# A residual layer with split float32 products: quarters in longer runs over two queues, the bias put into the bank ahead of the products, tiles 2 to 7 turned by VectorE

## The chip, the core and the metric

The kernel runs on one core of a Trainium2 chip. A core has TensorE (the matmul array, which writes into the eight banks of PSUM), VectorE, ScalarE and GpSimd for elementwise work, SyncE, which issues transfers, and 16 DMA engines that all transfers share. Each engine works through its own instructions in order; semaphores hold an instruction until what it needs is done. The metric is the device time of one execution in microseconds (us); of a version, the median of its runs.

## The reference: what is computed

x has shape (4, 1024, 512), the condition (4, 256), W (1536, 512), b (512). Cut to what matters:

```python
hidden = concatenate([cond, cond], -1)                       # (4, 512)
x_mean = mean(x, axis=1, keepdims=True)                      # (4, 1, 512)
fused  = concatenate([x, x_mean * ones, hidden * ones], -1)  # (4, 1024, 1536)
y      = x + relu(einsum('bld,do->blo', fused, W) + b)
```

The einsum falls into three: x times the first 512 rows of W (the large product), the mean of x over the 1024 positions times the next 512 rows, and the condition times the last 512, whose two halves can be added first. The second and third parts and b are the same for all 1024 positions of a row of the batch: they are called the row's bias here. The output is x + relu(product + bias).

## The kernel before

The 4 x 1024 positions are 32 tiles of 128 positions, eight per row. For the product TensorE needs x turned, with the features along the partitions. Tiles are grouped into ten units: tiles 0 and 1 alone, tiles 2 and 3, tiles 4 to 7, and then units of four tiles, two per row. A unit's features come in four pieces of 128 (j = 0 to 3).

*Turning.* Units 0 to 3 (tiles 0 to 7, `BY_PE`) are turned by TensorE: x is loaded with positions along the partitions, and `nc.tensor.transpose` (L261) writes 128x128 blocks into PSUM. The other six units are loaded a second time as "z", in an arrangement (`zv`, L119) that puts each quarter of the features on 32 partitions, so that VectorE's transpose of 32x32 blocks (L267) finishes the turn. A z unit is eight transfers of 128 KB (half h, quarter i, L161), and each of its runs in memory is 64 floats, 256 bytes.

*Splitting.* The product is kept at float32 accuracy by splitting each operand into a float32r part and the rest: `hi` is ScalarE's copy (L278, which also sums over positions for the mean), `lo` is VectorE's or GpSimd's subtraction (L294). W's first part is split in the same way (L237 to L245). For each tile and piece, TensorE then does three matmuls, w_hi x hi, w_hi x lo, w_lo x hi (L439), so 12 per tile, into one of five banks (`O_BANKS`).

*The bias.* ScalarE scales the condition's W rows (L356), GpSimd adds them (L361), ScalarE copies the sum into a bank (L365), VectorE adds four mean terms to it (L368) once the row's sums are there, the result is split (L374, L378), TensorE multiplies it with a matrix of 1/1024 so as to sum over the partitions (L385), and ScalarE copies the row's bias out (L389).

*Finishing.* The first five tiles (`KEEP = 5`) are copied out of their bank by ScalarE before the bias exists (L451), and GpSimd adds the bias later (L457). For the others VectorE adds the bias while it reads the bank (L457), ScalarE applies relu (L460), GpSimd adds x (L463). The last four tiles are done by VectorE alone: bias into the bank (L473), then relu and x in one operation (L468). The last tile is done in two halves of 256 columns. Each tile is stored by L478.

*What sets the order.* The class `Plan` (L18) is a list scheduler that runs while the program is built: every operation has an engine with a cost, the operations it depends on, and a due time; the plan takes the operation that could start first, by due time within a small window, and emits it. So each engine's order, SyncE's order of loads and stores too, comes out of these costs. The due times follow `at(t)`, the time planned for tile t. On the chip each engine keeps that order and waits where data are late. All loads of x, z and W and all stores are issued by SyncE on one queue. Eight semaphores serve the transfers in turn, so a transfer is issued only when the eighth before it has landed.

*The start.* Five matmuls on zeros (L225) run first. Tile 0's x, the first half of W, tile 1's x, the second half of W, the rest of unit x0 and x1, w_mean and w_cond are issued in this order, then the z units.

Of the kernel before, what the change touches and what calls it, by code (L numbers as in the profile page):

```python
# [8 lines left out]
F32 = mybir.dt.float32  # L9
# [8 lines left out]
class Plan:  # L18
# [3 lines left out]
    HANDOVER = 0.2  # L22
    PATIENCE = 0.12

    def __init__(self, engines):
        self.free = dict.fromkeys(engines, 0.0)
        self.todo, self.done, self.log = {}, {}, []

    def add(self, key, costs, deps, due, emit, later=0.0):
        assert key not in self.todo, key  # L30
        self.todo[key] = (costs, list(deps), due, emit, later)

    def run(self):
        while self.todo:
            could = []
            for key, (costs, deps, due, _, _) in self.todo.items():
                if not all(d in self.done for d in deps):
                    continue
                options = []
                for engine, cost in costs.items():  # L40
                    start = self.free[engine]
                    for d in deps:
                        end, later, by = self.done[d]
                        if by != engine:
                            end += later + self.HANDOVER
                        start = max(start, end)
                    options.append((start + cost, start, engine, cost))
                _, start, engine, cost = min(options)
                could.append((start, due, key, engine, cost))
            assert could, list(self.todo.items())[:8]  # L50
            first = min(could, key=lambda t: t[:2])
            start, _, key, engine, cost = min(
                (t for t in could if t[3] == first[3] and t[0] <= first[0] + self.PATIENCE),
                key=lambda t: (t[1], t[0]),
            )
            _, _, _, emit, later = self.todo.pop(key)
            self.log.append((start, engine, key, start - self.free[engine]))
            self.free[engine] = start + cost
            self.done[key] = (start + cost, later, engine)
            emit(engine)  # L60
# [3 lines left out]
def kernel(  # L64
# [8 lines left out]
    nc = tc.nc  # L73
# [11 lines left out]
    S_BUFS = 13  # L85
    T_BUFS = 3
# [3 lines left out]
    O_BUFS = 14  # L90
    KEEP = 5
    BY_DVE = 3
# [3 lines left out]
    STEP, START = 2.82, 6.0  # L96
# [17 lines left out]
    plan = Plan(["pe", "dve", "act", "pool", "sp"])  # L114
    nc_of = {"pe": nc.tensor, "dve": nc.vector, "act": nc.scalar, "pool": nc.gpsimd}
# [3 lines left out]
    zv = x.rearrange("r (n t) (h i c) -> r h i t n c", t=Q, i=NQ, h=2)  # L119
    Wv = W.rearrange("(s h p e) o -> s h p e o", p=P, e=2, h=2)  # L120
# [4 lines left out]
    BY_PE = (0, 1, 2, 3)  # L125
# [8 lines left out]
    in_sbuf = {c for c, (u, js) in enumerate(pieces) if u not in BY_PE and js[0] == 3}  # L134


    xs, zs = {}, {}
# [15 lines left out]
    def x_here(t):  # L153
        return ("x", t // G, t % G) if t < 2 else ("x", 0, 2) if t < G else ("x", t // G)

    def load_z(u, h, i):
        r, k0, n = units[u]
        if not h and not i:
            zs[u] = zpool.tile([P, 2, G * NQ, P // 2], F32, tag="z", name=f"z{u}")
        i = (0, 2, 1, 3)[i]  # L160
        nc.sync.dma_start(  # L161
            out=zs[u][i * Q : (i + 1) * Q, h, : n * NQ],
            in_=zv[r, h, i, :, k0 * NQ : (k0 + n) * NQ],
        )

    def load_w(h):
        nc.sync.dma_start(out=w_x[:, 2 * h : 2 * h + 2], in_=Wv[0, h])

    SP, SPZ = 0.7, 1.3
    clock = 1.9  # L170
    for key in (("x", 0, 0), ("w", 0), ("x", 0, 1), ("w", 1), ("x", 0, 2), ("x", 1)):
        if key[0] == "w":
            load_w(key[1])
            clock += 2 * SP
        else:
            n = 1 if key in (("x", 0, 0), ("x", 0, 1)) else 2 if len(key) == 3 else G
            load_x(key[1], key[2] if len(key) == 3 else 0, n)
            clock += n * SP
        plan.done[key] = (clock, 0.3, "sp")
    plan.free["sp"] = clock  # L180
# [7 lines left out]
    wcs = {}  # L188
    plan.add(("w_mean",), {"sp": 4 * SP}, [("x", 1)], -50, lambda e: nc.sync.dma_start(out=w_mean.rearrange("p (h e) o -> p h e o", h=2), in_=Wv[1].rearrange("h p e o -> p h e o")), later=1.0)
    for n, u in enumerate(by_z):  # L190
        for h in range(2):
            for i in range(NQ):
                deps = [("turn", c) for c in range(len(pieces)) if n >= Z_BUFS and pieces[c][0] == by_z[n - Z_BUFS]]
                due = at(first_tile[u]) - 30 + i + 4 * h if u != 3 else -60
                plan.add(("z", u, h, i), {"sp": SPZ / 2}, deps, due, lambda e, u=u, h=h, i=i: load_z(u, h, i), later=1.0)
    x_order = ["w_x", 0, 1, "cond"] + list(range(2, B * NK // G))
    for n, g in list(enumerate(x_order))[3:]:
# [29 lines left out]
    for _ in range(N_WARM):  # L227
        warm_up()
# [340 lines left out]
```

## Time and profile before

| what | us |
|---|---|
| median of 3 runs (115.6 to 117.58) | 115.7 |
| the profiled execution | 114.52 |
| its span in the profile | 112.7 |
| TensorE busy, matmuls (443) | 102.3 |
| VectorE busy (131 operations) | 73.0 |
| GpSimd busy (62) | 68.6 |
| ScalarE busy (123) | 54.0 |
| transfers, share of the 16 DMA engines' time over the span | 84.6% |
| bytes read and written | 17.83 MB and 8.39 MB |

Busy time of matmuls counts overlapping instructions, each from its start to its modelled end. Successive starts tell the pace better. An idle stretch of an engine is put down to what ended it. Stretches of time are read in slices of the span; a share of an engine or of the transfers there says what that stage was short of. By line, the matmuls of the product are 150 us of such overlapping spans, the transposes by TensorE 6.4, the matmuls of the mean 3.4.

### The profile page before, as it was taken

What the parts mean: (1) busy time and instruction counts of PE and PEld (TensorE: products, weight loads), DVE (VectorE), ACT (ScalarE), POOL (GpSimd) and SP (SyncE); (2) the same over time, 40 slices, a digit from 0 to 9 for tenths busy, and PEclk for the clock granted to TensorE, in tenths of its full rate; (3) what the DMA queues carried; (4) which work ended last, traced back from release to release, by engine and by line L of the source; (5) the groups of instructions that cost most, each with busy time, mean ns of one, the idle gap of its engine ahead of it and who ended that gap; (6) DMA issues with size and microseconds to landing.
All of it is one profiled execution on the core that took longest, in us unless ns stands there. A gap on an engine that the chain in (4) does not pass through costs nothing.

```text
span 112.7 us, 1479 instructions
## 1 busy us (share of the span) xinstructions
PE 102.3 (91%) x443; PEld 80.7 (72%) x443; DVE 73.0 (65%) x131; ACT 54.0 (48%) x123; POOL 68.6 (61%) x62
## 2 busy tenths in 40 slices
PE   5879999999999999989999899999993499999970
PEld 2447888888887888858888588888881488888860
DVE  1299245568969999898975993699049442224470
ACT  5260357799849850999542473662216522220000
POOL 6159007299979999799999948575506744440000
PEclk9999999999999999999999999999999999999997
DMA  3999999999999989999999999999893222224231
GB/s 104 338 351 400 405 331 181 187 133 192 221 317 174 197 229 329 345 215 341 377 257 209 282 386 307 307 310 333 202 333 111 93 93 93 93 93 186 93 128 59
DMA packets 35487, 26.31 MB, mean 233 GB/s; under 512 B 26132, under 2 KB 26392, under 8 KB 35480
## 3 DMA queue, kind: packets, MB, share of 16 engines
q1 hardware_dynamic: 35440, 26.22, 84.6%
q8 instruction: 3, 0.05, 0.2%
q14 instruction: 4, 0.03, 0.1%
q0 software_dynamic: 32, 0.00, 0.0%
q10 hardware_dynamic: 8, 0.00, 0.0%
HBM read 17.83 MB, written 8.39 MB: 233 GB/s over the span
## 4 chain that ended last, share of the span: by engine, by line
PE 35%; POOL 21%; DMA 20%; DVE 9%; issue 5%; ACT 4%; SPq 2%; POOLq 0%
PE po_None L439 26%; DMA out_dram<-o 11%; POOL o L463 10%; DMA z<-in_x_dram 9%; POOL o L457 5%; PE xT L261 4%; POOL cond L361 3%; POOL lo L294 3%; PE po L439 3%; ACT hi L278 2%; PE pw L225 2%; DVE xT L267 2%; SPq L478 2%; DVE w_lo L244 2%; DVE acc L368 1%
## 5 line engine op out<-in xcount | busy, mean ns | idle before, releaser
L439 PE MATMUL po_None<-w_hi,lo 128*128 128x512 f32 x124 | 50.1, 404 | 0.6 <-POOL lo L294 0.6
L439 PE MATMUL po_None<-w_hi,hi 128*128 128x512 f32 x124 | 50.6, 408 | 0.0
L439 PE MATMUL po_None<-w_lo,hi 128*128 128x512 f32 x124 | 49.6, 401 | 0.7 <-DVE w_lo L244 0.7
L463 POOL TENSOR_TENSOR o<-o,x 128x512 f32<-128x512 f32 x28 | 35.8, 1292 | 12.9 <-ACT o L460 8.3
L278 ACT ACTIVATE hi<-xT 128x512 fp32r<-128x512 f32 (+1 forms) x34 | 19.5, 575 | 20.3 <-DVE xT L267 9.7
L439 PEld LDWEIGHTS po_None<-w_lo,hi 128*128 128x128 f32 x124 | 23.7, 191 | 7.1 <-DVE w_lo L244 1.4
L439 PEld LDWEIGHTS po_None<-w_hi,lo 128*128 128x128 f32 x124 | 23.9, 192 | 6.4 <-POOL lo L294 1.0
L439 PEld LDWEIGHTS po_None<-w_hi,hi 128*128 128x128 f32 x124 | 23.9, 193 | 5.3
L294 DVE TENSOR_TENSOR lo<-xT,hi 128x512 fp32r<-128x512 f32 (+1 forms) x28 | 17.9, 643 | 8.3 <-ACT hi L278 8.3
L460 ACT ACTIVATE o<-o 128x512 f32<-128x512 f32 x28 | 16.8, 628 | 11.9 <-DVE o L457 11.9
L267 DVE STREAM_TRANSPOSE xT<-z 128x512 f32<-128x512 f32 x24 | 16.1, 702 | 9.2 <-DMA z<-in_x_dram 7.2
L457 DVE TENSOR_TENSOR o<-po_None,bias 128x512 f32<-128x512 f32 x23 | 15.2, 681 | 9.4 <-POOL o L463 4.2
L368 DVE SCALAR_TENSOR_TENSOR acc<-w_mean,tot,acc 128x512 f32<-128x512 f32 x16 | 12.1, 755 | 0.5
L294 POOL TENSOR_TENSOR lo<-xT,hi 128x512 fp32r<-128x512 f32 x6 | 7.8, 1294 | 4.7 <-ACT hi L278 4.7
L457 POOL TENSOR_TENSOR o<-o,bias 128x512 f32<-128x512 f32 x5 | 6.4, 1310 | 1.0 <-ACT bias L389 1.0
L261 PE MATMUL xT<-ident,x 128*128 128x128 f32 x32 | 6.4, 327 | 0.4 <-DMA x<-in_x_dram 0.4
L261 PEld LDWEIGHTS xT<-ident,x 128*128 128x128 f32 x32 | 5.4, 206 | 1.6 <-DMA x<-in_x_dram 0.8
L347 POOL TENSOR_TENSOR wc<-w_cond 128x512 f32<-128x512 f32 x2 | 2.5, 1287 | 6.6 <-DMA w_cond<-in_L_cond_W_dram 6.6
L361 POOL TENSOR_TENSOR cond<-b_sb,term 128x512 f32<-128x512 f32 x4 | 5.2, 1294 | 2.1 <-ACT term L356 2.1
L278 ACT ACTIVATION_READ_ACCUMULATOR hi<-xT 128x1 f32 x32 | 6.2, 195 | 0.0
L361 POOL TENSOR_TENSOR cond<-cond,term 128x512 f32<-128x512 f32 x4 | 5.2, 1298 | 0.2
L356 ACT ACTIVATE term<-wc,cT 128x512 f32<-128x512 f32 x8 | 5.3, 714 | 0.0
(46 smaller groups left out, 56.2 us busy)
## 6 DMA issues: line engine op xcount, KB each, us to landing
out_dram<-o SPq DMA_DIRECT2D x31, 256.0 KB, 4.4
x<-in_x_dram SPq DMA_DIRECT2D x7, 1024.0 KB, 7.1
z<-in_x_dram SPq DMA_DIRECT2D x48, 128.0 KB, 5.2
w_x<-in_L_cond_W_dram SPq DMA_DIRECT2D x2, 512.0 KB, 4.5
w_mean<-in_L_cond_W_dram SPq DMA_DIRECT2D x1, 1024.0 KB, 10.9
w_cond<-in_L_cond_W_dram SPq DMA_DIRECT2D x1, 1024.0 KB
x<-in_x_dram SPq DMA_DIRECT2D x2, 256.0 KB, 3.2
x<-in_x_dram SPq DMA_DIRECT2D x1, 512.0 KB, 6.3
```

The costliest lines, as they stand in the source:

```text
L261: nc.tensor.transpose(v[:, (m * n + i) * P : (m * n + i + 1) * P], x_t[:, j // 2, j % 2], ident)
L267: nc.vector.transpose(v[:, : n * P].rearrange("p (n t) -> p n t", t=Q), zs[u][:, js[0] // 2, : n * NQ].rearrange("p n (a e) -> p n e a", e ...
L278: nc.scalar.activation(hi[c][:, :m], xT[c][:, :m], AF.Copy, accum_out=sums[:, r, js[0], s : s + 1] if len(js) == 1 else None,)
L294: nc_of[e].tensor_tensor(lo[c][:, :m], xT[c][:, :m], hi[c][:, :m].bitcast(F32), ALU.subtract)
L347: eng.tensor_tensor(wc[:, k], v[:, 0, k], v[:, 1, k], ALU.add)
L356: nc.scalar.activation(terms[r, n], wc[:, n], AF.Copy, scale=cT[:, n, r : r + 1])
L361: nc.gpsimd.tensor_tensor(conds[r], conds[r] if n else bL, terms[r, n], ALU.add)
L368: nc.vector.scalar_tensor_tensor(acc[r], w_mean[:, j, :], totals[r][:, j : j + 1], acc[r], ALU.mult, ALU.add)
L439: nc.tensor.matmul(pos[key][:, :w], lhsT=v[p][:, c], rhs=m[:, j, d], start=(j == 0 and n == 0), stop=(j == J - 1 and n == 2),)
L457: nc_of[e].tensor_tensor(o, o if t < KEEP else pos[t], biases[t // NK], ALU.add)
L460: nc.scalar.activation(outs[t], outs[t], AF.Relu)
L463: nc_of[e].tensor_tensor(outs[t], outs[t], x_tile(t), ALU.add)
```

## The change

The new version keeps the three matmuls per piece and the arithmetic. What differs:

- **z in longer runs.** Features are dealt to pieces in another way: piece j takes features 128 i + 32 j + c, where c counts within 32. A z unit is then four transfers instead of eight, with runs of 128 floats, 512 bytes, and VectorE's transpose reads 32 neighbours per block instead of every second. W's rows are loaded in the same order, as four transfers per part (`load_w`). From unit 4 on, quarters 1 and 3 are issued by ScalarE, on its queue; the others stay with SyncE. The order of all loads is written out (`LOADS`), and each load depends on the load before it on each queue.
- **Tiles 2 to 7 by VectorE.** `BY_PE` holds only tiles 0 and 1. Units 2 and 3 become z units. For tiles 0 and 1 VectorE first copies x into the dealt order (`deal`), in two halves, and TensorE turns the copy.
- **lo.** GpSimd takes the lo of pieces 1 and 3 of every z unit, and all four of unit 2; VectorE takes the rest. w_lo is all VectorE's.
- **The bias ahead of the products.** For tiles 20 to 23 and 26 to 31 (`EARLY`) ScalarE copies the row's bias into the bank first (`preload`), the products add to it without a start flag, and VectorE does relu and x in one operation. Other tiles go as before; `KEEP` is 3 and the parked tiles are finished later.
- **Row 0's bias** begins with the first mean term; the condition's part is added at the end (`acc_end`).
- **Fillers.** Where the plan leaves TensorE idle for over 0.2 us before the condition's transposes, matmuls on zeros of 128 columns are put in: six before tile 0's transposes, eight before the first product, one before tile 2. The condition's transposes move behind tile 2's first piece.
- **The plan** has other costs, models the transfers as one line with bytes, and adds to each due time a shift by kind and a random part from a fixed seed. The buffer counts change.

The diff, cut to its core:

```diff
-    S_BUFS = 13
-    T_BUFS = 3
+    S_BUFS = 14
+    T_BUFS = 4
-    O_BUFS = 14
-    KEEP = 5
-    BY_DVE = 3
+    O_BUFS = 10
+    KEEP, PARKED = 3, 5.0
+    IN_SBUF = {2: (0, 1, 2, 3), 3: (1, 3)}
+    EARLY = (99, 16, 20, 26)
+    TWO, Z_MB = 4, 3.8
+    SEED, SPREAD, SHIFT = 27816, 1.0, {
...
-    zv = x.rearrange("r (n t) (h i c) -> r h i t n c", t=Q, i=NQ, h=2)
-    Wv = W.rearrange("(s h p e) o -> s h p e o", p=P, e=2, h=2)
+    zv = x.rearrange("r (n t) (i f) -> r i t n f", t=Q, i=NQ)
+    Wv = W.rearrange("(s i j c) o -> s j i c o", i=NQ, j=J, c=Q)
-    BY_PE = (0, 1, 2, 3)
+    BY_PE = (0, 1)
-    in_sbuf = {c for c, (u, js) in enumerate(pieces) if u not in BY_PE and js[0] == 3}
+    in_sbuf = {c for c, (u, js) in enumerate(pieces) if u not in BY_PE and js[0] in IN_SBUF.get(u, (1, 3))}
...
-        nc.sync.dma_start(
-            out=zs[u][i * Q : (i + 1) * Q, h, : n * NQ],
-            in_=zv[r, h, i, :, k0 * NQ : (k0 + n) * NQ],
+        nc_of[e].dma_start(
+            out=zs[u][i * Q : (i + 1) * Q, : n * NQ], in_=zv[r, i, :, k0 * NQ : (k0 + n) * NQ]
         )
+    LOADS = [("z", 2), ("z", 3), ("cond",), ("w_mean",), ("z", 4), ("z", 5), ("x", 0), ("x", 1)]
+    for u, g in zip(range(6, len(units)), range(2, B * NK // G)):
+        LOADS += [("z", u), ("x", g)]
+            for i in range(NQ):
+                load(("z", u, i), "act" if i % 2 and u >= TWO else "sp", Z_MB * units[u][2] / 16, frees[v],
+                     at(first_tile[u]) - 22 + i, lambda e, _, u=u, i=i: load_z(e, u, i))
...
+            if not conds_turned and idle > 0.2:
+                for _ in range(int((idle - 0.1) / 0.1)):
+                    warm_up(P)
...
+    def deal(t, h):
+        if not h:
+            dealt[t] = small.tile([P, J, P], F32, tag="term", bufs=TERMS, name=f"dealt{t}")
+        j = slice(h * J // 2, (h + 1) * J // 2)
+        nc.vector.tensor_copy(
+            dealt[t][:, j].rearrange("p j (q c) -> p j q c", q=NQ),
+            x_tile(t).rearrange("p (q j c) -> p j q c", q=NQ, j=J)[:, j],
+        )
...
-            nc.vector.transpose(
-                v[:, : n * P].rearrange("p (n t) -> p n t", t=Q),
-                zs[u][:, js[0] // 2, : n * NQ].rearrange("p n (a e) -> p n e a", e=2)[:, :, js[0] % 2],
+                zs[u][:, : n * NQ, js[0] * Q : (js[0] + 1) * Q],
             )
...
+    def acc_end(r):
+        nc.vector.tensor_tensor(acc[r], acc[r], conds[r], ALU.add)
+    def preloaded(t):
+        return t >= EARLY[t // NK]
+    def preload(t, h):
+        nc.scalar.activation(bank(t, h), biases[t // NK][:, cols(h)], AF.Copy)
...
-                start=(j == 0 and n == 0), stop=(j == J - 1 and n == 2),
+                start=(i == 0 and not preloaded(t)), stop=(i == 3 * J - 1), skip_group_check=preloaded(t),
...
-    def bias_in_bank(t, h=None):
-        nc.vector.tensor_tensor(v, v, biases[t // NK][:, d], ALU.add)
+    def relu_add_x(t, h):
+        d = cols(h)
+        nc.vector.scalar_tensor_tensor(o_tile(t)[:, d], bank(t, h), 0.0, x_tile(t)[:, d], ALU.max, ALU.add)
```

## The prediction, made before the changed kernel was run

> **What bounds the kernel now.** I read the slices first, then TensorE's timeline, then the chain of waits at the one large hole. The slices (40 of 2.82 us):
>
> ```profile
> PE   5879999999999999989999899999993499999970
> PEclk9999999999999999999999999999999999999997
> DMA  3999999999999989999999999999893222224231
> GB/s 104 338 351 400 405 331 181 187 133 192 221 317 174 197 229 329 345 215 341 377 257 209 282 386 307 307 310 333 202 333 111 93 93 93 93 93 186 93 128 59
> ```
>
> TensorE is full but for both ends and one hole near 87 us. The transfers are full too until about 82 us, and at the full share they move 400 GB/s in some slices and 133 to 200 in others: those are the quarters, in runs of 256 bytes. So TensorE sets the end, and where it stops it is for data that came late. Products follow each other at 0.233 us once the array is fast (72 in 16.79 us in the chain that ended last), but not at first:
>
> ```profile
> 8.71 0.63 PE L439 MATMUL po_None<-w_hi,hi 128*128 128x512 f32 x1
> 9.14 0.63 PE L439 MATMUL po_None<-w_hi,lo 128*128 128x512 f32 x1
> 9.57 0.63 PE L439 MATMUL po_None<-w_lo,hi 128*128 128x512 f32 x1
> ...
> 12.59 0.39 PE L439 MATMUL po_None<-w_hi,hi 128*128 128x512 f32 x1
> 12.82 0.39 PE L439 MATMUL po_None<-w_hi,lo 128*128 128x512 f32 x1
> 13.05 0.40 PE L439 MATMUL po_None<-w_lo,hi 128*128 128x512 f32 x1
> ```
>
> Starts lie 0.43 us apart before 12.6 us and 0.23 after, although the column of the granted clock reads 9 throughout. The hole, in time order over all engines:
>
> ```profile
> 76.85 0.42 SPq L161 DMA_DIRECT2D z<-in_x_dram  x1
> 83.41 1.30 DVE L267 STREAM_TRANSPOSE xT<-z 128x512 f32<-128x512 f32 x2 [4.38 <-DMA z<-in_x_dram]
> 85.13 0.40 PE L439 MATMUL po_None<-w_lo,hi 128*128 128x512 f32 x1
> 88.09 0.68 DVE L378 TENSOR_TENSOR acc_lo<-acc,acc_hi 128x512 fp32r<-128x512 f32 x1
> 88.83 0.50 PE L385 MATMUL pb<-acc_hi,mean 128*128 128x512 f32 x1 [3.30 <-DVE acc_lo L378]
> ```
>
> The last quarter of the last unit is issued at 76.85, behind the store of tile 19, which waited for GpSimd; VectorE turns it at 83.41, the last row's mean follows, and TensorE, which takes its work in order, stands before the mean's product (the row reads 3.30; start to start it is 3.70 less one slot, 3.47).
>
> **The sum from the front.** The 25th product (tile 2's first) starts at 16.57 and the last ends at 109.18. From there TensorE has 29 tiles x 12 x 0.2333 = 81.2, the last tile 2.84, twelve transposes at 0.117 = 1.4, four mean products of two slots (1.9), the hole 3.5: 90.8 of 92.6; the other 1.8 are short gaps.
>
> *Start.* Tile 0's x is there by 3.87 (its transposes start). New ahead of them are two half copies on VectorE (a whole 128x512 copy takes 0.43 there, so 0.5 with the gap); then four transposes at the slow 0.27, ScalarE's hi 0.60, and eight filler matmuls of 128 columns (a quarter of 0.43 each, 0.85) that stand in order before the first product: 3.87 + 0.5 + 1.1 + 0.85 = 6.3, against 6.20 now. W in quarters does not bring the first 1.5 MB sooner (ScalarE waited until 7.54 for the last of it, same order of bytes), but w_lo is now all VectorE's: 0.68 each, where one took 1.79 beside GpSimd's. From 6.3 to tile 2 TensorE has 24 products and four transposes. Fast: 24 x 0.2333 + 4 x 0.117 = 6.1, tile 2 at 12.4. Slow until 12.6 as now: 12 products by then, 12 x 0.2333 = 2.8 left, 15.4. The fillers close the gaps that TensorE has now (5.01 to 5.42, 7.40 to 8.12), so I take the middle, 13.9. The rule of the Trainium skill (TensorE: Matmul & The Clock Gate, Part 1) is that about 3.4 us of sustained activity release the clock; the trace is slower than that, being busy from 1.18 with small gaps and slow until 12.6. By the rule tile 2 would start near 12.4.
>
> *Data for tiles 2 to 7.* Now TensorE turns these from x; now 24 transposes fall away, 2.8 us, but their quarters must land early. What does a run of 512 bytes cost? No row shows one. Bounds:
>
> ```profile
> 8.50:14.10 5.60, 5.60 (x21) 4.46 (x21) 3.53 (x6) 1.09 (x4) 2.56 (x2) 1.00 1.03 401
> ...
> 22.50:25.40 2.90, 2.90 (x14) 2.36 (x13) 1.78 (x3) 2.64 (x6) 2.82 (x3) 1.00 0.96 132
> 25.40:28.20 2.80, 2.80 (x13) 2.26 (x13) 2.53 (x4) 2.80 (x9) 2.53 (x3) 1.00 0.91 195
> ```
>
> The last column is GB/s: quarters alone move 132 to 195, say 170; rows of 2 KB and more 345 to 401, say 375. A straight line through time per run (16 engines: 24 ns for 256 bytes, 87 for 2 KB) gives 33 ns for 512, **248 GB/s**; ends 170 and 375. The Trainium skill (DMA: Bandwidth & Descriptors, Specifications) gives 512 B as the least transfer for full rate; by that it is 375 and all below is 2.7 us earlier. Its front page (Trainium Kernel Development and Optimization, Key Constraints) says that a second queue saves issue time alone; no run here shows two.
>
> Unit 3 (tiles 4 to 7): 1.5 MB by 7.5, then units 2 and 3 and the two quarters of unit 4 that ScalarE issues early, 2.0 MB, 8.1 us: 15.6. Its first lo stands on VectorE behind four turns (0.65 each), a sum and totals: 15.6 + 3.4 + 0.7 = 19.7. TensorE reaches tile 4 at 13.9 + 5.6 + 0.3 (condition's transposes, moved here) = 19.8: no wait. Its second lo is GpSimd's, behind the two adds that need w_cond, another 1 MB: 15.6 + 2.8 + two of 1.28 + 1.29 = 22.3; in order TensorE wants it after two slots of three products, 21.2. So **1.3 us of new wait** (handover counted). At 375 none; at 170 the two waits come to 4.7.
>
> *After that.* The transposes (1.4 of them past 16.57), the hole (3.5) and the short gaps (1.8) are gone if the data are early: tile 28's unit is issued behind nine stores instead of twenty, and all 8 units' loads are 7.9 MB at 248 = 32 us, with 10.6 MB of the rest at 375 = 28, some 63 us of transfers against a need near 80. TensorE: 13.9 + 81.2 + 2.84 + 1.9 + 0.34 + 1.3 = 101.5.
>
> *Tail.* From the last product to the span's end is 3.55 now. The bias now lies in the bank, so one of two VectorE halves goes (109.21 to 109.67, 0.46): 3.09. Preloading costs ScalarE ten copies of 0.60 and 0.38, hidden: they run up to a bank ahead of the products, and six relus of 0.63 and two copies out of banks leave. Uncovered, a preload costs 0.6 per tile.
>
> *Engines.* ScalarE 54.0 + 5.6 - 3.8 - 1.2 = about 55 and twelve issues; VectorE 73 - 7 (lo) - 5.7 (bias) + 4.4 (turns) + 4.2 (relu and x) + 3 = about 72; GpSimd adds eight lo at 1.29 and four halves, loses six x adds, two bias adds, two w_lo: 69. None nears 100.
>
> Span 101.5 + 3.1 = 104.6; the profiled execution lies 1.8 over its span (114.52 to 112.7): **106.4 against 114.52**. The median shown is 115.7, 1.2 higher, so the same 8.1 off it is 107.6. I say 107.0.
>
> **Rivals.**
> (A) *The banks run out.* Only tiles 0 to 2 are parked by ScalarE instead of 0 to 4, so tiles 3 to 7 hold all five banks until row 0's bias exists. By rows: w_cond at 18.8, four GpSimd operations to 23.9, two adds 26.5, add, hi and lo 28.7; TensorE wants it at 29.5 and tile 3's bank at 32.8. Margin one to two us. Against: now the first bias add ends at 34.66 (start 33.98); no better than that costs 1.9, and the same again for row 1's bias, whose product stands inside tile 12: 2 to 5 in all, 109 to 112.
> (B) *The hole moves.* Row 3's mean product stands after tile 25's first slot; if unit 9 lands as late as now relative to TensorE, 3.5 comes back, with A's first part 110 to 113.
> (C) *Slower: ScalarE is held by its issues.* Twelve loads now stand in ScalarE's order, and a load waits at issue for the eighth before it. On SyncE:
>
> ```profile
> L161 SPq DMA_DIRECT2D z<-in_x_dram x48: 423/652/5882, 4.6 to 76.8; - x48
> ```
>
> (minimum, median, maximum in ns.) The first 18 took 23.19 us, 1.3 each. ScalarE has some 30 us free until unit 9's hi, so 2.5 us per issue hide; beyond it every hi behind is late. At 3.5 each: 12 us, 118.6. At the median 0.65 nothing; at the worst 5.88, 40. Against: the same bytes come in half as many runs, so the eighth load before has landed sooner.
> (D) *The clock stays slow until 12.6*: tile 2 at 15.4, but unit 3's second lo at 22.3 binds either way, so 0.2 only. And the second queue may bring nothing; in the sum it brings nothing.
>
> **How the numbers follow.** Forecast (103.6 to 109): 0.63. A 0.18, B 0.11, C 0.05, others 0.03. Range 103.6 (375 GB/s, fast start, profile's scale) to 111.5 (170 GB/s or A, the median's scale); outside lie most of B and C. Within 2% means 113.4 to 118, about what a measurement can tell from none: the tops of A and B, 0.07; slower 0.05; faster 0.88.
>
> **What would show it.** Right: tile 2's first product at 12.4 to 15.4; no transposes of 128x128 after it but the condition's; a wait of one to two us on GpSimd's lo near 21; slices with quarters at 220 to 300 GB/s; mean products without a hole; one VectorE operation after the last product. Wrong: the quarters still at 170, ScalarE's issue rows over 2.5 us, waits of products for VectorE's bias adds near 33 or 47 (A), a hole before the fourth mean product (B).

## The result: 141.75 us, slower by 22%

| version | median, us | runs |
|---|---|---|
| before | 116.64 | 4 (115.6 to 119.4) |
| the change | 141.75 | 4 (140.85 to 142.31) |

The ratio is 1.2249, with a 95% interval of 1.2133 to 1.2365. The forecast was 107.0, in a range of 103.6 to 111.5. The profiled execution took 141.47 us, its span 139.7 (forecast: 104.6). Runs of one version spread by several us (the kernel before lies between 110.38 and 119.4 over all series below), so a difference within that spread is not taken as shown.

The slices of the changed kernel (40 of 3.49 us; busy tenths, then GB/s):

```profile
PE   6624439996599002999999999999960999999990
DMA  3453669995555999999899999999999745051132
GB/s 83 141 157 114 133 142 210 226 207 133 133 143 137 201 203 188 180 204 274 228 236 312 160 333 260 277 274 289 303 402 405 302 166 224 0 225 75 75 150 75
```

Where the kernel before was full from the first slices on, TensorE now has holes at 8 to 20 us, at 44 to 56 and near 105. In the first 20 us the transfers move 83 to 157 GB/s with the engines 0.3 to 0.6 busy; before, 338 to 405 at full share from 2.8 to 14.1 us. So the stage is short of data while about half of the DMA engines' time is idle. TensorE's rows after its longest waits, in order of time:

```profile
11.75 0.79 PE L570 MATMUL po_None<-w_hi,hi 128*128 128x512 f32 x1 [2.85 <-ACT w_hi L310]
15.63 0.80 PE L570 MATMUL po_None<-w_hi,hi 128*128 128x512 f32 x1 [2.24 <-ACT w_hi L310]
19.89 0.79 PE L570 MATMUL po_None<-w_hi,hi 128*128 128x512 f32 x1 [2.61 <-ACT w_hi L310]
...
54.96 0.77 PE L490 MATMUL pb<-acc_hi,mean 128*128 128x512 f32 x1 [9.68 <-DVE acc_lo L483]
...
108.22 0.49 PE L570 MATMUL po_None<-w_hi,hi 128*128 128x512 f32 x1 [4.63 <-ACT po_None L558]
```

The first three rows lie 3.9 and 4.3 us apart. Each waits for one quarter of W, 256 KB: ScalarE's copies of them start at 11.07, 14.95 and 19.21, each released by a load of w_x. That is 62 to 68 GB/s per load. The copy of the last part of W, in the kernel before and in the changed one:

```profile
7.54 0.63 ACT L237 ACTIVATE w_hi<-w_x 128x512 fp32r<-128x512 f32 x1 [0.36 <-DMA w_x<-in_L_cond_W_dram]
```

```profile
19.21 0.63 ACT L310 ACTIVATE w_hi<-w_x 128x512 fp32r<-128x512 f32 x1 [3.63 <-DMA w_x<-in_L_cond_W_dram]
```

The same pitch comes back in VectorE's mean terms, which lead to the hole of 9.68:

```profile
36.10 0.75 DVE L470 TENSOR_SCALAR acc<-w_mean,tot 128x512 f32<-128x512 f32 x1 [4.29 <-DMA w_mean<-in_L_cond_W_dram]
...
40.27 0.76 DVE L472 SCALAR_TENSOR_TENSOR acc<-w_mean,tot,acc 128x512 f32<-128x512 f32 x1 [2.69 <-DMA w_mean<-in_L_cond_W_dram]
44.04 0.76 DVE L472 SCALAR_TENSOR_TENSOR acc<-w_mean,tot,acc 128x512 f32<-128x512 f32 x1 [3.01 <-DMA w_mean<-in_L_cond_W_dram]
48.36 0.76 DVE L472 SCALAR_TENSOR_TENSOR acc<-w_mean,tot,acc 128x512 f32<-128x512 f32 x1 [3.56 <-DMA w_mean<-in_L_cond_W_dram]
```

Against the forecast's account of TensorE, the 35.1 us divide so. Tile 2's first product starts at 25.90 instead of 13.9: 12.0. After it TensorE stands idle 1.91, 0.92, 9.68 and 4.63, in all 17.1, where 1.3 was forecast: 15.8. After the holes 25 products start 0.43 apart instead of 0.233 (granted clock 0.50 from 54 to 61 us, 0.98 from 61 to 64): 4.9. The tail is 0.2 longer than forecast. Some 2.2 is in short gaps that I did not follow up.

The hole of 4.63 is not one of a load of W. VectorE had waited for quarters until 102.03, and the copy of the bias into the bank (L558) stands on ScalarE behind a `hi` whose transpose came late:

```profile
102.03 1.90 DVE L358 STREAM_TRANSPOSE xT<-z 128x512 f32<-128x512 f32 x3 [5.88 <-DMA z<-in_x_dram]
106.99 0.60 ACT L369 ACTIVATE hi<-xT 128x512 fp32r<-128x512 f32 x1 [2.90 <-DVE xT L358]
107.57 0.59 ACT L558 ACTIVATE po_None<-bias 128x512 f32<-128x512 f32 x1
```

### The profile page after: what moved, and what is told of

It reads as the page before. It is cut to its first block, busy times and chain, and to the rows that moved or that the text cites. A ratio compares the mean times of both kernels' runs of the same rounds, so it can differ in the third digit from the quotient of the medians.

```text
span 139.7 us, 1454 instructions
## 1 busy us (share of the span) xinstructions
PE 108.3 (78%) x434; PEld 83.5 (60%) x434; DVE 68.6 (49%) x130; ACT 54.4 (39%) x126; POOL 68.7 (49%) x64
## 3 DMA queue, kind: packets, MB, share of 16 engines
q10 hardware_dynamic: 6344, 3.15, 11.6%
## 4 chain that ended last, share of the span: by engine, by line
DMA 62%; PE 20%; SPq 10%; DVE 3%; issue 2%; ACT 1%; DVEq 0%
DMA z<-in_x_dram 41%; PE po_None L570 18%; DMA w_mean<-in_L_cond_W_dram 13%; DMA out_dram<-o 8%; SPq L205 7%; PE po L570 2%; SPq L211 2%; DVE xT L358 1%; SPq L192 1%; DVE o L585 1%; DVE acc L472 1%; DVE lo L383 0%; ACT po_None L558 0%; PE pb L490 0%; DVE o L595 0%
## 5 line engine op out<-in xcount | busy, mean ns | idle before, releaser
L570 PE MATMUL po_None<-w_hi,hi 128*128 128x512 f32 x124 | 52.8, 429 | 14.3 <-ACT w_hi L310 7.7
L570 PEld LDWEIGHTS po_None<-w_hi,hi 128*128 128x128 f32 x124 | 25.2, 203 | 22.4 <-ACT w_hi L310 9.1
L383 POOL TENSOR_TENSOR lo<-xT,hi 128x512 fp32r<-128x512 f32 (+1 forms) x18 | 20.8, 1165 | 26.6 <-ACT hi L369 26.6
L591 POOL TENSOR_TENSOR o<-o,x 128x512 f32<-128x512 f32 x22 | 28.0, 1292 | 11.1 <-ACT o L588 7.0
L358 DVE STREAM_TRANSPOSE xT<-z 128x512 f32<-128x512 f32 (+1 forms) x32 | 20.1, 661 | 14.2 <-DMA z<-in_x_dram 13.9
L585 DVE TENSOR_TENSOR o<-po_None,bias 128x512 f32<-128x512 f32 x19 | 12.4, 681 | 10.0 <-ACT bias L494 5.5
L588 ACT ACTIVATE o<-o 128x512 f32<-128x512 f32 x22 | 13.0, 621 | 2.0 <-DVE o L585 2.0
L595 DVE SCALAR_TENSOR_TENSOR o<-po_None,x 128x512 f32<-128x512 f32 x9 | 6.2, 687 | 11.7 <-PE po_None L570 9.6
L383 DVE TENSOR_TENSOR lo<-xT,hi 128x512 fp32r<-128x512 f32 x16 | 10.8, 673 | 0.0
L490 PE MATMUL pb<-acc_hi,mean 128*128 128x512 f32 x4 | 2.0, 506 | 9.7 <-DVE acc_lo L483 9.7
L310 ACT ACTIVATE w_hi<-w_x 128x512 fp32r<-128x512 f32 x3 | 1.9, 629 | 12.3 <-DMA w_x<-in_L_cond_W_dram 12.3
## 6 DMA issues: line engine op xcount, KB each, us to landing
z<-in_x_dram SPq DMA_DIRECT2D x16, 256.0 KB, 11.5
z<-in_x_dram ACTq DMA_DIRECT2D x12, 256.0 KB, 11.6
w_cond<-in_L_cond_W_dram SPq DMA_DIRECT2D x1, 1024.0 KB, 11.5
```

What stands on the lines that cost most here:

```text
L358: nc.vector.transpose(v[:, : n * P].rearrange("p (n t) -> p n t", t=Q), zs[u][:, : n * NQ, js[0] * Q : (js[0] + 1) * Q],)
L383: nc_of[e].tensor_tensor(lo[c][:, :m], xT[c][:, :m], hi[c][:, :m].bitcast(F32), ALU.subtract)
L570: nc.tensor.matmul(po, lhsT=v[p][:, c], rhs=m[:, j, cols(h)], start=(i == 0 and not preloaded(t)), stop=(i == 3 * J - 1), skip_group_check ...
L585: nc_of[e].tensor_tensor(o, o if t < KEEP else bank(t), biases[t // NK], ALU.add)
L588: nc.scalar.activation(outs[t], outs[t], AF.Relu)
L591: nc_of[e].tensor_tensor(outs[t], outs[t], x_tile(t), ALU.add)
```

## The experiments

Two theories to begin with. **Theory 1**: the loss is in the loads of W. `load_w` reads W as "s j i c o", so each load's source consists of four blocks of 32 rows; such a load runs on a few engines only, and whatever is queued behind it on those engines waits. **Theory 2**: the loss is in the quarters of x, in their 512-byte runs on two queues, which land late (a median of 11.5 us after issue, 5.2 before).

### W cut into loads of 32 partitions

```diff
+    Wq = W.rearrange("(s i j c) o -> s i c j o", i=NQ, j=J, c=Q)
-        nc.sync.dma_start(out=v[:, j], in_=Wv[s, j])
+        if s:      # w_mean: four loads, 32 partitions x 4 pieces
+            nc.sync.dma_start(out=v[j * Q : (j + 1) * Q], in_=Wq[s, j])
+        elif j % 2 == 0:      # w_x: eight loads, 32 partitions x 2 pieces
+            for i in range(NQ):
+                nc.sync.dma_start(out=v[i * Q : (i + 1) * Q, j : j + 2], in_=Wq[s, i, :, j : j + 2])
```

Same bytes, same places; the source's outer dimension is now 32 rows. Then each half of the cut alone.

> The changed kernel, with each load of W cut so that its outer dimension is 32 rows in place of 4 blocks (w_x in eight loads of 32 partitions by two pieces, w_mean in four of 32 partitions by four pieces); same bytes, same place in the queue. T1 (a load whose outer dimension is 4 is served by few DMA engines, and everything behind it in the queue waits): W lands in 3 us instead of 12, w_mean without 4 us between quarters, 104 to 110 us in all. T2 (it is the quarters of z, in 512-byte runs over two queues, that land late, 11.5 us instead of 5.2): only the first waits shrink, 125 us or more.

> Only w_x is cut to 32 rows, w_mean stays in four loads of 4 blocks. T1: tile 2's first product comes near 14 in place of 25.9, the hole before row 0's mean product (9.7) stays or grows because TensorE gets there sooner: 122 to 132 us. T2: 130 or more.

> Only w_mean is cut, w_x stays in four loads of 4 blocks. T1: the start stays late (tile 2 near 26), the hole of 9.7 goes: 120 to 130 us. T2: 135 or more.

Both cut: **119.31** (118.6 to 121.69), 1.0476 times the kernel before, interval 1.0326 to 1.0627. That takes 22.4 us off. W alone gives 134.15, w_mean alone 133.89 (two runs each; 1.1803, interval 1.1605 to 1.2, and 1.178, interval 1.1524 to 1.2037). Each alone brings 8, both 22: with W early, TensorE meets the late w_mean sooner (its hole is 11.60 there). All three lie above what theory 1 had put on them (104 to 110, 122 to 132, 120 to 130). So theory 1 is right in direction and too small: 119 is not 107, some 12 us are still missing.

### The same loads in the kernel before

```diff
-    Wv = W.rearrange("(s h p e) o -> s h p e o", p=P, e=2, h=2)
+    Wv = W.rearrange("(s i j c) o -> s j i c o", i=NQ, j=J, c=Q)
-        nc.sync.dma_start(out=w_x[:, 2 * h : 2 * h + 2], in_=Wv[0, h])
+        for j in (2 * h, 2 * h + 1):
+            nc.sync.dma_start(out=w_x[:, j], in_=Wv[0, j])
```

w_mean likewise. W's rows then no longer belong to the features beside them, so it is another product of the same size.

> The kernel before, with W and w_mean loaded in quarters of 4 blocks as the changed kernel does, and nothing else (W's rows then do not match the features, so another product of the same size is computed). T1: W lands 12 us late and the z loads behind it too: 128 to 142 us. T2: within 2 us of before.

**136.91** (two runs; ratio 1.2045, interval 1.1846 to 1.2245), 22.2 us above the kernel before in that series (114.7). With the quarters of x as they were, this one part makes nearly the whole loss, which decides against theory 2 as its main cause. Tile 1's x, which is no part of the edit, is waited for 7.14 us there (0.42 before), and its transposes start at 12.15 instead of 5.42: what stands behind such a load is late as well.

```profile
12.15 1.13 PE L266 MATMUL xT<-ident,x 128*128 128x128 f32 x4 [7.14 <-DMA x<-in_x_dram]
```

### Loads alone

A kernel that only loads, 1 MB per stage, each stage closed by VectorE; it computes nothing of the reference.

> Loads alone, 1 MB per stage, each stage ended by VectorE; it computes nothing of the reference. Stages: rows of x, 2 KB runs on 128 partitions; W in four quarters of four blocks; W with rows 4p + j, 2 KB runs on 128 partitions; W in 2 KB runs with each load onto 32 partitions; quarters of x in 512-byte runs, each load onto 32 partitions, on one queue; the same on two queues; eight loads in 256-byte runs; 512-byte runs on 128 partitions. Theory 1: the second stage takes some 13 to 16 us where the first and third take 3 to 4. If a load onto 32 partitions is limited by where it writes, the fourth, fifth and sixth stages all take 4.5 to 5.5 us (190 to 235 GB/s) and the eighth with the same run length 3 to 4; if the run length decides, the fourth takes 3 to 4 and the eighth as long as the fifth. If two queues bring bandwidth, the sixth is shorter than the fifth by 15% or more.

Its slices (1.9 us each), the stages one after the other:

```profile
DMA  0960022222200691069301990029700896009900
GB/s 11 297 243 0 0 50 99 103 99 103 94 3 0 211 288 53 0 207 253 92 0 43 265 230 13 0 79 320 153 0 0 204 238 109 0 0 286 266 4 0
```

| stage (1 MB) | first packet to end of last, us | GB/s |
|---|---|---|
| rows of x, 2 KB runs, 128 partitions | 3.73 | 281 |
| W in four quarters of four blocks | 11.57 | 91 |
| W with rows 4p + j, 2 KB runs, 128 partitions | 4.26 | 246 |
| W, 2 KB runs, each load onto 32 partitions | 4.41 | 238 |
| quarters of x, 512-byte runs, 32 partitions, one queue | 4.64 | 226 |
| the same on two queues | 4.56 | 230 |
| in eight loads of 256-byte runs | 4.98 | 211 |
| 512-byte runs, 128 partitions | 3.93 | 267 |

In the stage of four blocks the digits of the DMA share are 2 throughout and the rate is 94 to 103 GB/s in full slices: about a quarter of the engines work, at 84 ns for 2 KB as in the first stage. The stage's packets take 46.1 us together, which is 4.0 engines over 11.57 us. It takes 2.7 times as long as the same bytes with 128 rows outermost (I had expected 13 to 16 us; alone it is 11.6, in the kernel these engines carry other loads too).

The Trainium skill (DMA: Bandwidth & Descriptors, "Why a DMA increments its semaphore by 16 and not by 1") says that a DMA is spread over the largest number of engines up to 16 that divides the outermost dimension larger than one of both its patterns. For 128 partitions and four blocks that is four, as the 4.0 engines' worth of packets shows. The prediction overlooked this rule.

The other stages fall into a narrow band. This is one execution, and the first and third stage, alike in runs and partitions, differ by 14%, so smaller differences between stages are not told apart. Doubling the run from 256 to 512 bytes saves 7% and the second queue 2%; neither is the 46% (170 to 248) that the prediction put on it. The expectation that a load onto 32 partitions is limited whatever its runs is not shown either: 2 KB runs lose 3% by it, 512-byte runs 15%, about as much as the spread just named.

### Rows 4p + j: all 128 partitions and 512-byte runs

```diff
-    Wv = W.rearrange("(s i j c) o -> s j i c o", i=NQ, j=J, c=Q)
+    Wv = W.rearrange("(s p j) o -> s j p o", p=P, j=J)
-                zs[u][:, : n * NQ, js[0] * Q : (js[0] + 1) * Q],
+                zs[u][:, : n * NQ].rearrange("p n (c j) -> p n c j", j=J)[:, :, :, js[0]],
```

> The changed kernel with another deal of the features: piece j takes features 4p + j on partition p, so that W, w_mean and the dealt rows of x keep 128 partitions and a source whose outer dimension is 128; the quarters keep their 512-byte runs and two queues, the plan is the same one, and the sum is the reference's. VectorE's transposes and the deal of tiles 0 and 1 read every fourth element. If W's loads over four blocks are what costs (theory 1), W is complete near 9 us instead of 19 and w_mean needs some 3 us instead of 15; what is left against my forecast are quarters at about 200 GB/s: 108 to 114, faster than the kernel before or level with it. If the loads onto 32 partitions, that is the quarters, are a large part of the loss (theory 2), it stays at 118 or above, near the 119.3 of the run with W in single quarters.

**124.84** (122.46 to 127.93; the kernel before in that series 117.13), a miss: above the 119.31 of the 32-partition cut, though W comes at full width (the kernel before, too, was 2.4 higher in this series). The group of VectorE's transposes there, and in the changed kernel:

```profile
L357 DVE STREAM_TRANSPOSE xT<-z 128x512 f32<-128x512 f32 (+1 forms) x32 | 31.8, 1029 | 10.8 <-DMA z<-in_x_dram 7.9
```

```profile
L358 DVE STREAM_TRANSPOSE xT<-z 128x512 f32<-128x512 f32 (+1 forms) x32 | 20.1, 661 | 14.2 <-DMA z<-in_x_dram 13.9
```

Busy time and mean ns stand behind the bar: reading every fourth element costs 1.09 us for 128x512 instead of 0.70 (the means mix a smaller form), 11.7 us of VectorE in all. In the kernel before, which reads every second element, it is 0.70. My experiment had repaired one cost and bought another; how much of the miss those 11.7 us make is not shown, since the kernel before with 512-byte runs, below, bears 9.6 more without a loss.

The Trainium skill (SBUF — State Buffer, "Door 1: The DMA port swizzle") has a note that SBUF has lines of 16 bytes and that full bandwidth needs at least two hits per line. Two hits are left at every second float32 element and one at every fourth, and that is where the step lies here, 0.70, 0.70 and 1.09. The same note gives "4 fp32" as how far one can stride for free; read as every fourth element, that does not agree with the 1.09, and the measurement decides.

> The run above with all quarters issued by SyncE, none by ScalarE. If the second queue only takes issue time off SyncE, the time is within 2 us of the run above. If the second queue brings bandwidth, quarters alone move 20% slower and the time is 3 us or more above it; if ScalarE's issues hold its other work up (rival C of the prediction), it is 2 us or more below.

With `TWO = 99` SyncE issues all quarters: **126.16** (123.79 to 127.18), level with 124.84. The second queue brings no bandwidth that shows.

### 512-byte runs alone, on the kernel before

The same edit of `zv` and of the transposes in the kernel before, W in 4 KB runs of rows 4p + 2h + e.

> The kernel before with one part of the change alone: its z units in four loads of 512-byte runs instead of eight of 256 bytes (features 4p + j on partition p, so that W keeps 128 partitions, 4 KB runs), all on SyncE. If 512-byte runs at 248 GB/s are worth what the prediction reckoned, the last unit lands some 4 us earlier and the hole before the last mean product shrinks from 3.5 to near nothing: 3 to 5 us faster. If loads onto 32 partitions are limited whatever their runs: within 2 us of the kernel before.

**114.88** (113.56 to 115.78) against 117.13 (114.18 to 118.78): 2.3 us by the medians, between the two expectations, but the runs of the two overlap, so a gain is not shown. Nor is a loss, although VectorE's transposes cost 9.6 us more there (25.7 for 16.1). In its trace the hole before the last mean product is gone, and waits of 1.92 at 6.91 and 2.10 at 67.50 have come, the span being 113.2 (112.7 before). What the longer run is worth is less than reckoned.

### The rest of the change with the loads of the kernel before

The old deal of the features comes back: W in halves on 128 partitions, quarters in eight loads of 256-byte runs, transposes of every second element. All else stays changed, but for tile 1's x, now issued between W's halves, and the plan's cost of an issue, halved for the quarters. Then the same with the plan told what the loads take, and its shifts and seed searched again; and this search for the 32-partition cut.

```diff
-    zv = x.rearrange("r (n t) (i f) -> r i t n f", t=Q, i=NQ)
-    Wv = W.rearrange("(s i j c) o -> s j i c o", i=NQ, j=J, c=Q)
+    zv = x.rearrange("r (n t) (h i c) -> r h i t n c", t=Q, i=NQ, h=2)
+    Wv = W.rearrange("(s h p e) o -> s h p e o", p=P, e=2, h=2)
...
-    TWO, Z_MB = 4, 3.8
+    TWO, Z_MB = 4, 5.2      # second run
```

> The changed kernel with the first part of the change undone: features dealt as in the kernel before, z units in eight loads of 256-byte runs, W and w_mean in halves of 4 KB runs on 128 partitions, VectorE's transposes reading every second element; the bias ahead of the products, tiles 2 to 7 by VectorE, the two queues and the plan's costs stay (an issue of a z load counts half in the plan, since there are twice as many). It computes the reference. If the loss lies in how W and w_mean are loaded and the rest of the change is worth what the prediction reckoned less the run length, 108 to 113, faster than the kernel before. If the rest of the change is itself a loss (tiles 2 to 7 wait for their quarters, or the banks run out, rival A), 116 to 124.

> The run above with the plan told what the loads take on the chip (quarters 5.2 us for a MB where it had 3.8) and its shifts and seed searched again under that cost. Same operations, another order. If what is left of the loss is the order (operations standing behind one that waits for a load the plan took to be there), this is 3 us or more faster than the run above, 105 to 110. If it is the rate of the loads itself, within 2 us of it.

> The first run of this study (the change, W cut by 32 partitions, 119.3 us) with the plan told what the loads take there (4.6 us for W's MB, 4.8 for one of quarters) and searched again. If the 12 us by which that run missed the forecast are the order alone, 107 to 112; if they are the rate of loads onto 32 partitions, 116 to 120.

**124.16** (123.28 to 125.13), **121.71** (116.68 to 122.79) and **120.77** (120.2 to 121.62), with the kernel before at 117.14 (111.66 to 118.89). In the first and third of them every run is above every run of the kernel before: with its own order the rest of the change is itself a loss, 7 us by the medians. How much of it is the order stays open: with the order searched again three runs lie at 121.67 to 122.79, but the fourth at 116.68. For the 32-partition cut a new order gains nothing that shows (119.31 before, in another series). TensorE's rows after waits in the first of these runs:

```profile
21.42 0.50 PE L568 MATMUL po_None<-w_hi,hi 128*128 128x512 f32 x1 [1.04 <-ACT hi L367]
22.99 0.49 PE L568 MATMUL po_None<-w_hi,lo 128*128 128x512 f32 x1 [1.07 <-DVE lo L381]
27.98 0.49 PE L568 MATMUL po_None<-w_hi,hi 128*128 128x512 f32 x1 [2.86 <-ACT hi L367]
29.33 0.80 PE L568 MATMUL po_None<-w_hi,lo 128*128 128x512 f32 x1 [0.86 <-POOL lo L381]
59.34 0.50 PE L568 MATMUL po_None<-w_hi,hi 128*128 128x512 f32 x1 [3.86 <-DVE o L583]
```

Tiles 4 to 7, now turned from quarters, are waited for in the first four of them, 5.8 us. VectorE turns their pieces from 17.57 and from 21.00 on, behind 1.37 and 2.70 of waiting for z. Ahead of the fifth ScalarE had stood 4.83 us at an issue until 51.58; row 1's bias came at 56.73 (44.98 in the kernel before), and VectorE freed the bank with it. The wait of 2.86 has one more cause, in ScalarE's timeline:

```profile
23.53 3.63 ACTq L205 DMA_DIRECT2D z<-in_x_dram  x2
27.21 0.63 ACT L367 ACTIVATE hi<-xT 128x512 fp32r<-128x512 f32 x1 [5.83 <-DMA w_mean<-in_L_cond_W_dram]
```

ScalarE has a z load to issue and stands 5.83 us until w_mean has landed; the `hi` behind it in its order, whose data were there, waits with it. That is rival C's mechanism. The issue's own row does not contain the wait.

### Tiles 2 to 7 back on TensorE

The run with the searched plan, with `BY_PE = (0, 1, 2, 3)`, transposes reading x as in the kernel before, no `deal`, the rows of x for tiles 2 to 7 first among the loads, and its order searched with the same costs.

> The run with the features dealt as before and the order searched again (121.7 us), with tiles 2 to 7 turned by TensorE from rows of x as in the kernel before, and its order searched with the same cost of the loads; the bias ahead of the products, the second queue and KEEP = 3 stay. It computes the reference. If what is left of the loss (4 to 7 us against the kernel before) is that tiles 2 to 7 now wait for 1.5 MB of quarters which land at 160 to 200 GB/s where rows land at 345 to 405, this gives 110 to 115: no wait of TensorE over 1 us between 20 and 32 us, and the last unit as early as there. If it is the rest (the banks with KEEP = 3, the order), 118 or more.

**116.94** (10 runs, 115.6 to 118.56; ratio to the kernel before 1.0004, interval 0.9957 to 1.0052), by the medians 4.8 us less than with the quarters; but that version's one run at 116.68 is as low. The expectation's 110 to 115 is missed by 2, and there is one hole, of 4.67 at 21.45: ScalarE stood 3.24 us at 20.55, by the same view as above, again "<-DMA w_mean" at an issue, and 3.79 at 16.72 on w_cond. So in the usual run, turning tiles 2 to 7 from quarters costs 4.8 us net where the prediction saved 2.8 of TensorE's transposes; in the trace with the quarters TensorE waits 1.96 and 3.39 between 24 and 31 us. That the issues on ScalarE eat what the rest of the change gains is argued from the hole of 4.67, and no run here takes them away from this version alone.

### The parts alone on the kernel before

Second queue (quarters 1 and 3 from unit 5 on), bias ahead of the last four tiles, and both:

```diff
-  plan.add(("z", u, h, i), {"sp": SPZ / 2}, deps, due, lambda e, u=u, h=h, i=i: load_z(u, h, i), later=1.0)
+  plan.add(("z", u, h, i), {"act": 0.1} if i % 2 and u > 4 else {"sp": SPZ / 2}, deps, due,
+           lambda e, u=u, h=h, i=i: load_z(e, u, h, i), later=...)
...
-        nc.vector.tensor_tensor(v, v, biases[t // NK][:, d], ALU.add)
+        nc.scalar.activation(v[:, : d.stop - d.start], biases[t // NK][:, d], AF.Copy)   # ahead of the products
```

> The kernel before with one part of the change alone: from unit 5 on, z quarters 1 and 3 are issued by ScalarE on its own queue, so they no longer stand behind stores on SyncE, and the last unit's loads stand ahead of nine stores more than now. It computes the reference. By the prediction's reading of the hole at 87 us (the last quarters issued behind stores that wait for GpSimd), 3 to 4 us faster than the kernel before. If the loads are late because the transfers are full until 82 us whoever issues them, within 1.5 us; if ScalarE is held by its issues (rival C), 2 us or more slower.

> The kernel before with another part alone: for the last four tiles ScalarE copies the bias into the bank ahead of the products, and VectorE does relu and x in one operation where it did two. It computes the reference. By the prediction's tail (one of two half operations of 0.46 us goes): 0.3 to 0.6 us faster, within the measurement; if the copies of 0.6 us are not hidden, 1 to 2.5 us slower.

> The kernel before with the two parts together that the two runs of them alone hold, the second queue and the bias ahead of the last four tiles. If the parts add up: the sum of the two, 3 to 4.5 us faster than the kernel before.

Second queue: **115.21** (113.65 to 116.24), ratio 0.9791, interval 0.9681 to 0.99, by the interval 1 to 3% faster than the kernel before in that series. Bias ahead: 115.37 (111.65 to 117.02) against 116.6, too wide to tell. Both: **114.85** (114.32 to 116.04), ratio 0.9832, interval 0.9759 to 0.9905; the parts do not add up to more than the queue alone. In the second-queue run the hole at 87 us is gone, 3.5 us, but ScalarE's and TensorE's timelines show a new one:

```profile
48.81 2.63 ACTq L161 DMA_DIRECT2D z<-in_x_dram  x2
51.48 0.60 ACT L280 ACTIVATE hi<-xT 128x512 fp32r<-128x512 f32 x1 [6.49 <-DMA z<-in_x_dram]
...
52.07 0.59 ACT L391 ACTIVATE bias<-pb 128x512 f32<-128x512 f32 x1
```

```profile
53.44 0.80 PE L441 MATMUL po_None<-w_hi,hi 128*128 128x512 f32 x1 [2.83 <-DVE o L459]
```

ScalarE stands 6.49 us at an issue until an earlier z load has landed; row 1's bias copy comes at 52.07 where it came at 44.98 before, VectorE adds it late, and TensorE finds no free bank for 2.83 us. Rivals C and A, in one chain.

### The last quarters earlier, without a second queue

```diff
-                due = at(first_tile[u]) - 30 + i + 4 * h if u != 3 else -60
+                due = at(first_tile[u]) - 40 + (i + 4 * h) / 8 if u != 3 else -60
```

The first quarter of a unit falls due 10 us earlier, its last 16. The last quarter of z then stands behind 11 stores on SyncE where it stood behind 20 (the expectation miscounts both); in the third run (- 50) behind 7. The second and third run add the bias ahead of the last four tiles.

> The kernel before with its z loads due 10 us earlier in the plan, all still on SyncE: the last unit's last quarter then stands ahead of 23 stores where it stood ahead of 15. No other engine issues loads. It computes the reference. If the gain of the second queue was only that late quarters no longer stand behind stores, and its loss the ScalarE work held by its issues (6.2 us near 45 us, after which TensorE waited 2.0 to 2.8 us for a bank), this keeps the first without the second: the hole near 87 us gone and none near 53, 3 to 4 us faster than the kernel before. If the quarters of one unit only take the transfers from other units, within 1.5 us.

> The run above with the bias ahead of the products for the last four tiles, as in the run of that part alone: 0.3 to 1.2 us faster than the run above.

> The run above with the z loads due 20 us earlier than in the kernel before: the last unit's last quarter stands ahead of 28 stores. If earlier is free, within 1 us of the run above; if quarters that come too early take the transfers from rows of x and from w_cond, a hole appears before 50 us and it is slower by 1 us or more.

**111.0** (110.78 to 112.41), **110.72** (110.09 to 111.8) and 113.59 (112.7 to 114.44); the kernel before in that series 116.88, six of its seven runs between 115.6 and 118.78 and one at 110.38. By the medians that is 5.9 us, but that one run is as low as the new version's best, and what made it so is not known: the gain holds against the usual run of the kernel before, not against its best. TensorE's row of the first run's slices (2.72 us each):

```profile
PE   5879999999999999799999999999999999999960
```

After the start (a wait of 1.09 at 6.09) TensorE has no hole left; the one dip is a wait of 0.60 at 44.12. The last quarters are issued up to 65.4 us (76.85 before), and row 3's mean product goes through at 78.5 without a wait. So the hole was the loads' place in SyncE's order; the span is 108.7 where the trace of the kernel before had 112.7, and 3.5 of those 4.0 are the hole. Too early costs again: with - 50 TensorE waits 0.65 at 40.89 for row 0's mean and 1.80 at 43.42 for a bank that VectorE frees with row 0's bias; w_cond, which that bias needs, is issued at 19.74 there, behind eleven z loads, and at 4.10 in the kernel before. The version with - 40 and the bias ahead has the lowest median of all, 110.72; against 111.0 without it the bias ahead adds nothing that shows.

## Why the prediction was wrong, step by step

**Start: the step that failed.** "W in quarters does not bring the first 1.5 MB sooner (ScalarE waited until 7.54 for the last of it, same order of bytes)" priced the new loads of W and w_mean by their bytes. By their shape they take 3.8 to 4.3 us per 256 KB in the kernel, W until 19.2 instead of 7.5, w_mean until 48. The first product came at 7.76 (forecast 6.3), tile 2's at 25.90 (12.4 to 15.4); with W cut it came at 16.60. The two runs with W cut and with the old W loads exchanged put 22 us on it, from both sides. None of the rivals had it: the only part of the change that the prediction doubted was the second queue, which "may bring nothing".

**What a run of 512 bytes costs** was mis-sized: 248 GB/s was put on a line between the 256-byte and 2 KB rows of the kernel; alone, 512 bytes gives 226 and 256 bytes 211, and in the run with W cut the slices that hold quarters alone move 177 to 216. The 170 was read from slices of the kernel before that hold 256-byte runs alone; why these move 132 to 195 there and 211 in a kernel that only loads is not shown. In the run with W cut VectorE turned unit 3's first piece, which needs all four quarters, at 17.55 after 2.39 of waiting for them: 2 us behind the forecast's 15.6.

**Data for tiles 2 to 7.** "24 transposes fall away, 2.8 us" is true of TensorE, and the wait put against it, 1.3, was too small: 4.8 us net on the wrong side by the medians, with the reservation made above. The mean term that stands on VectorE ahead of its second `lo` of unit 3 did not appear in the sum; in the run with W cut, it waited 8.95 us for w_mean and TensorE 5.93 for the `lo` behind it.

**After that.** The hole before the last mean product is gone in the changed kernel, as forecast, though there TensorE comes to it 28 us later; it is gone too with W cut, and the run with the quarters due earlier shows its worth in one trace: a span of 108.7 against 112.7. It is the one large term that was right, and it needed no second queue. The copies of the bias ahead of the products, put at nothing as "hidden", were not hidden once: the hole of 4.63. And 32 and 28 us of transfers are 60, not "some 63", which changes nothing.

**The tail.** One VectorE operation follows the last product, as forecast (136.44). From the last product's start to the end of the span it is 3.58, against 3.81 before: 0.23 of the 0.46.

**Rivals.** C was given 0.05 and its mechanism is real: ScalarE stood 7.59 and 4.63 us at an issue in the changed kernel and 3 to 9.8 us in seven others. I had set it that low because half as many runs would land sooner, and named the wrong evidence for it: the issue rows stay at 0.32 us, the wait stands in the bracket of the next ScalarE row. A came in behind it in the run with the second queue alone. The slow pitch that D priced at 0.2 for the start came as 4.9 us after the holes. B did not come.

**Still open.** What makes up the 2.2 us of short gaps, why the order searched anew did not help the 32-partition cut, and why runs of one version differ by up to 8 us. Of the 12.2 us by which the span with W cut (116.8) exceeds the forecast, 2.7 are tile 2's late start and 6.0 the waits after it (7.3 for a forecast of 1.3); the rest is in part the slow pitch after the hole of 5.93. A second queue on an engine with no work of its own was not tried.

## What to carry to other kernels

Price a load by its shape before its bytes, and look at the outermost dimension of both sides: 4 there gave 91 GB/s here, 32 gave 238 and 128 gave 246. When transfers are put on a compute engine's queue, look for their waits in the rows behind them, since that engine's work stands still until a place is free. And where a hole ends on a late load, first ask what stands ahead of that load in its own queue; moving it there was the cheapest cure here, 116.88 to 111.0 us by the medians, with one run of the kernel before as low as 110.38.

## What was not expected of the hardware

- Four loads of 256 KB over four blocks of rows: 91 GB/s alone, 62 to 68 beside others, with a DMA share of 0.2; 246 with 128 rows outermost. Another load issued behind them let its tile start 6.7 us late.
- VectorE's 32x32 transposes of 128x512 float32: 0.70 us for neighbours and for every second element, 1.09 for every fourth.
- After a hole of 9.68 us the products ran 0.43 apart for 6 us with a granted clock of 0.50. At the start of the kernel before, the same pitch stands beside a granted clock of 1.00.
